# Two attention layers and an MLP on one core: pinning VectorE's waits, setting a PSUM tile aside earlier, and cutting filler work finer

## The chip, the cores and the metric

The kernel runs on one core of a Trainium2 chip. The metric is the time of one execution on the device, in microseconds. Before the change it is 3975.42 us, the median of three runs (3967.12, 3975.87 and 3975.42).

## What is computed

Sixteen images of 256 channels by 32x32 positions, all in fp32. Each goes through two blocks in turn; S = 1024 positions are the tokens.

```
layer 0:  qkv = xs @ w_proj + b_proj                 # 4 heads of 64
          attn = softmax(q k^T * 64**-0.5)
          x = (attn v) @ w_out + b_out + xs
layer 1:  h = group_norm(x)                          # 32 groups of 8 channels
          q, k, v = h @ qkv_w^T                      # 8 heads of 32
          attn = softmax(q k^T * 32**-0.5 + phys_bias)
          x = x + (attn v) @ proj_w^T + proj_b
          h = group_norm(x)
          x = x + mlp_w2 @ gelu(mlp_w1 @ h + mlp_b1) + mlp_b2     # 256 -> 1024 -> 256
```

The softmax is computed without subtracting a maximum: the kernel sums the exponentials, checks at the end that no denominator left a safe range, and would run a slower general pass if one had (it does not with these inputs). A weighted sum of v is scaled by the reciprocal of the denominator afterwards.

## The kernel before

An image lives in SBUF as two chunks of 128 channels by 1024 positions. Positions are taken in two halves of 512 (`TB`, index `t`), keys in eight blocks of 128 (`kb`).

**The first attention** (`attention_a`) has four items: two halves `t` by two pairs of heads `c`. Each item has eight units, one for each key block. A unit computes scores (`s_a`, line 296, four matmuls of 64x64 side by side), the exponential on ScalarE (`e_a`, line 304), and two units later the weighted sum (`acc_a`, line 318, four matmuls). VectorE adds up the exponentials (`es_a`, line 330) for the denominators. **The second attention** (`attention_b`) also has four items of eight units: scores of four heads (`s_b`, line 401, eight matmuls of 32x64), two exponentials (`e_b`, line 413), the weighted sum one unit later (`acc_b`, line 422, four matmuls of 128x32) and two additions on VectorE (`es_b`, line 439).

**PSUM.** Accumulators of even items, of the second attention, and its denominators come from a pool of two single banks (`bank`). Everything else comes from three tiles of two banks each, s0 to s2, handed out in turn by `wide`: scores, projections, pieces of qkv and MLP, group norm averages, denominators of the first attention. A new tile waits until all readers of the old one in the same place are done. The sums of the odd items of the first attention (`acc_a_1`, `acc_a_3`) take tile 2 as a whole: from their first `weigh` until their last, `kept` holds the number 2 and `wide` passes over it. By then the scores of the item's first three units have been handed out from all three tiles.

**Denominators.** `normalise` forms column sums with matmuls (`den_a`, line 348; `den_b`, line 454). `denominators` then copies them to SBUF on ScalarE (`d`), spreads them over partitions with a DMA (`sp`), takes reciprocals on VectorE (line 262), writes them to DRAM (`row`) and reads them back broadcast over partitions (`rd`). VectorE multiplies the weighted sums by what came back (lines 367 and 469), after which the output projection `o` or `j` can run.

**Order of work.** The program is written as one stream. A small planner, `Later`, holds functions that fall due after a number of steps; it ticks once for each unit or piece. `run` steps through an attention and may run one filler piece after a unit, from the dictionary `fill`. In an image the order is: first attention; first MLP product (`hidden`, m<-gn_h, line 676) of the image before; the first half of q and k and all of v of the second attention; second attention, with filler pieces between its units: the rest of q and k (4 pieces at units 0, 1, 2, 4), the second MLP product of the image before (`reduce`, m<-g; 8 pieces, each 8 products over 256 positions), and q, k, v of the next image's first attention (12 pieces). During attentions `product` cuts a 128-column matmul into four of 32 columns (`cols`), which run side by side. The group norm before the MLP (`gm_h`, `gv_h`, lines 533 to 565) of an image falls into the next image's first attention, with the second output projection `j_1` ahead of it.

A scheduler under the kernel then fixes the order of instructions in each engine's queue. It keeps the dependencies, but may put an instruction ahead of others on its engine when it takes its input to be ready sooner, DMA transfers included. Waits are semaphores set by the producing engine.

Names used below: `x` the image (updated in place), `res_a`, `res_b` the weighted sums, `rd_a`, `rd_b` the transferred reciprocals, `sp_a`, `sp_b` the spread denominators, `inv` their reciprocals, `mean_c`, `dv`, `tv`, `rstd` steps of the group norm, `gn_g`, `gn_h` its two results.

Of the kernel before, what the change touches and what calls it, by code (L numbers as in the profile page):

```python
# [188 lines left out]
def first_pass(ctx, tc, x, out, k):  # L189
    nc = tc.nc  # L190
    B, C, S = x.shape
    CC, SB, NT = C // P, S // P, S // TB
    HC = k["w1"].shape[2] // P
    later = Later()
# [8 lines left out]
        tc.tile_pool(name="ps_a", bufs=2, space=bass.MemoryType.PSUM)  # L203
    )


    turn, kept = [0], set()

    dram = ctx.enter_context(
        tc.tile_pool(name="dram", bufs=4, space=bass.MemoryType.DRAM)  # L210
    )

    def wide(name, n=None):
        while n is None:
            if turn[0] not in kept:
                n = turn[0]
            turn[0] = (turn[0] + 1) % 3
        return ps_s.tile([P, 2, TB], F32, tag=f"s{n}", name=name)

    def bank(name):  # L220
# [29 lines left out]

    def denominators(key, d, n, waits, then):
        w = 4 * TB // P
        spread = work.tile([P, w], F32, tag="spread", name=f"sp_{key}", bufs=2)
        row = dram.tile([4 * TB // n, n], F32, tag="row", name=f"row_{key}", bufs=4)
        full = work.tile([P, CC * TB], F32, tag="full", name=f"rd_{key}", bufs=1)[:, :n]
        nc.sync.dma_start(spread, d[::32].rearrange("p (a b) -> p a b", b=w))

        def invert():  # L260
            inverse = work.tile([P, w], F32, tag="inverse", name=f"inv_{key}", bufs=2)
            nc.vector.reciprocal(inverse, spread)
            nc.sync.dma_start(row.rearrange("r (a b) -> (r a) b", b=w), inverse)
            nc.gpsimd.tensor_add(dsum, dsum, spread)
            nc.gpsimd.tensor_add(isum, isum, inverse)
            num = P * n // (4 * TB)
            for r in range(P // num):
                nc.sync.dma_start(
                    full[r * num : (r + 1) * num], row[r].partition_broadcast(num)
                )  # L270
            later.after(waits[1], lambda: then(full))

        later.after(waits[0], invert)
# [10 lines left out]
    def attention_a(b, qT, kT, v, project):  # L284
        key, D, lag = f"a_{b}", D0, 2
        items = [(t, c) for t in range(NT) for c in range(CC)]
        units = [(i, kb) for i in range(len(items)) for kb in range(SB)]
        res = act.tile([P, CC, S], F32, tag="res", name=f"res_{key}")
        accs, held, sums = {}, {}, {}

        def scores(i, kb):
            t, c = items[i]
            s = wide(f"s_{key}_{i}_{kb}")
            for g in range(2):
                for h in range(0, P, HALF):
                    nc.tensor.matmul(  # L296
                        s[h : h + HALF, g, :],
                        kT[g * D : (g + 1) * D, c, kb * P + h : kb * P + h + HALF],
                        qT[g * D : (g + 1) * D, c, t * TB : (t + 1) * TB],
                        start=True,  # L300
                        stop=True,
                    )
            e = work.tile([P, 2, TB], F32, tag="e", name=f"e_{key}_{i}_{kb}", bufs=8)
            nc.scalar.activation(e, s, AF.Exp, scale=float(D) ** -0.5)  # L304
            return i, kb, e

        def weigh(i, kb, e):
            t, c = items[i]
            if kb == 0:
                if i % 2:  # L310
                    kept.add(2)
                    acc = wide(f"acc_{key}_{i}", 2)
                    accs[i] = [acc[:, h, :] for h in range(2)]
                else:
                    accs[i] = [bank(f"acc_{key}_{i}_{h}") for h in range(2)]
            for h in range(2):
                for g in range(2):
                    nc.tensor.matmul(  # L318
                        accs[i][h][g * D : (g + 1) * D, :],
                        v[h * HALF : (h + 1) * HALF, kb, c * 2 + g],  # L320
                        e[h * HALF : (h + 1) * HALF, g, :],
                        start=(kb == 0),
                        stop=(kb == SB - 1),
                    )
            if kb == 0:
                held[i] = e
                return
            if kb == 1:
                sums[i] = work.tile([P, 2, TB], F32, tag="es", name=f"es_{key}_{i}", bufs=4)
            nc.vector.tensor_add(sums[i], held[i] if kb == 1 else sums[i], e)  # L330
            if kb == SB - 1:
                r = res[:, c, t * TB : (t + 1) * TB]
                one, two = accs.pop(i)
                nc.scalar.copy(r, one)
                nc.vector.tensor_add(r, r, two)  # L335
                kept.discard(2)
                if c == CC - 1:
                    later.after(1, lambda: normalise(t))


        def normalise(t):
            half = TB // 2
            den = wide(f"den_{key}_{t}")[:, 0, :]
            for c in range(CC):
                for g in range(2):
                    for h in range(2):
                        j = (2 * g + h) * 32
                        nc.tensor.matmul(
                            den[j : j + 32, c * half : (c + 1) * half],
                            k["ones"][:, :32],  # L350
                            sums[t * CC + c][:, g, h * half : (h + 1) * half],
                            start=True,
                            stop=True,
                        )
            denominators(
                f"{key}_{t}", den_copy(f"{key}_{t}", den), CC * TB,
                (2, 5) if t < NT - 1 else (1, 1),
                lambda full: scale(t, full),
            )

        def scale(t, full):
            r = res[:, :, t * TB : (t + 1) * TB]
            halves = [
                y.rearrange(form, c=CC, h=2)
                for y, form in ((r, "p c (h q) -> p c h q"), (full, "p (h c q) -> p c h q"))
            ]
            nc.vector.tensor_mul(halves[0], *halves)
            later.after(1 if t < NT - 1 else 4, lambda: project(t, res))

        cols[0] = 32  # L370
        pending = []
        for n, u in enumerate(units):
            pending.append(scores(*u))
            if n >= lag:
                weigh(*pending.pop(0))
            yield
        for p in pending:
            weigh(*p)
            if p is pending[-1]:
                cols[0] = P  # L380
            yield

# [5 lines left out]
    def attention_b(b, qT, kT, v, project):  # L388
# [5 lines left out]
        accs, held, sums = {}, {}, {}  # L394
# [55 lines left out]
        def normalise(i, r, last):  # L450
            t, c = items[i]
            den = bank(f"den_{key}_{i}")
            for g in range(G):
# [6 lines left out]
                )  # L460
            denominators(
                f"{key}_{i}", den_copy(f"{key}_{i}", den), TB,
                ((3, 5) if b + 1 < B else (1, 1)) if last else (2, 2),
                lambda full: scale(i, r, last, full),
            )

        def scale(i, r, last, full):
            t, c = items[i]
            nc.vector.tensor_mul(r, r, full)
            if c == CC - 1:  # L470
                wait = (10 if b + 1 < B else 1) if last else 1
                later.after(wait, lambda: project(t, res[t]))
# [195 lines left out]


    def mlp(b, xb, hn):  # L670
        gs = {}

        def hidden(t, hc):
            ps = wide(f"m1_{b}_{t}_{hc}")[:, 0, :]
# [9 lines left out]
            nc.scalar.activation(g, ps, AF.Gelu, bias=k["m1b"][:, hc : hc + 1])  # L684
            gs[t, hc] = g

        def reduce(t, co, half):
            n = TB // 2
            ps = wide(f"m2_{b}_{t}_{co}_{half}")[:, 0, :n]
            for hc in range(HC):  # L690
                product(
                    ps,
                    k["w2"][:, hc, co * P : (co + 1) * P],
# [1 line left out]
                    start=(hc == 0),  # L695
                    stop=(hc == HC - 1),
                )
            y = xb[:, co, t * TB + half * n : t * TB + (half + 1) * n]
            nc.vector.scalar_tensor_tensor(  # L699
                y, ps, k["m2b"][:, co : co + 1], y, ALU.add, ALU.add  # L700
            )
            if half:
# [5 lines left out]
        return (  # L708
            [lambda t=t, hc=hc: hidden(t, hc) for t in range(NT) for hc in range(HC)],
            [  # L710
                lambda t=t, co=co, half=half: reduce(t, co, half)
                for t in range(NT) for co in range(CC) for half in range(2)
            ],
        )


    def run(stage, fill=None):
        for n, _ in enumerate(stage):
            later.tick()
            if fill and n in fill:  # L720
                fill[n]()

    def run_pieces(pieces):
        for piece in pieces:
            piece()
            later.tick()

# [24 lines left out]
    for b in range(B):  # L754
# [16 lines left out]
        later.flush()  # L771
        tiles1, (qk, v) = qkv_1(b, xn[0])
        n = len(qk) // CC
        run_pieces(qk[:n] + v)
        fill = dict(zip((0, 1, 2, 4), qk[n:]))
        rest = outputs + (first if b > 0 else [])
        end = []
        if b == B - 1:

            rest, end = rest[:4], rest[4:]  # L780
        for m, piece in enumerate(rest):
            fill[5 + m * (last - 5) // (len(rest) - 1)] = piece
        hn = []
        run(
            attention_1(
# [312 lines left out]
```

## Time and profile before

| | |
|---|---|
| span of the profiled execution | 3973.2 us |
| TensorE (PE) busy | 3894.5 us, 98% |
| VectorE (DVE) busy | 2121.3 us, 53% |
| ScalarE (ACT) busy | 2044.0 us, 51% |
| mean granted TensorE clock | 0.995 |
| one image in the middle (476.53 to 722.89) | 246.36 us |
| of it: first attention, MLP's first product, front of qkv, second attention | 71.79, 31.51, 13.86, 129.20 us |

How to read it: the busy time of TensorE is the union of its matmuls' durations, and a matmul of which the end is modelled may seem to last until the next starts. The starts are exact, so a stage is best read by the distance of the starts of its groups. In a timeline, a row has start, duration, engine, line, operation, output<-inputs, tile of the array (rows*columns), shape and the number of records merged; in brackets stands the idle time before it and what ended it. One fp32 matmul appears as two records. Groups that run on different parts of the array overlap, so the durations of records add up to more than the time. "PEld" rows are weight loads, which run beside matmuls. In the list of waits a row has the engine, the waiting instruction, what it waited for, the total, the count and the longest.

### The profile page before, as it was taken

The numbers are of one execution on the slowest core, as the hardware profiler recorded it, in microseconds if no ns is written. First come the engines' busy times: TensorE is split into PE (matmuls) and PEld (weight loads), VectorE is DVE, ScalarE is ACT, GpSimd is POOL, SyncE is SP. The second block draws the span as 40 slices with busy tenths as digits, with TensorE's granted clock in tenths as the row PEclk, the third lists the DMA queues.
The fourth block names the chain that finished last, engine by engine and source line by source line (L and its number), as shares of the span: only waits on it lengthen the run. The fifth ranks groups of instructions, "written<-read, shape, count | busy, mean of one in ns | idle before, by whom it ended". The sixth has DMA issues, their size and how long they took to land.

```text
span 3973.2 us, 84589 instructions
## 1 busy us (share of the span) xinstructions
PE 3894.5 (98%) x37485; PEld 1461.6 (37%) x37485; DVE 2121.3 (53%) x2569; ACT 2044.0 (51%) x2369; POOL 93.9 (2%) x252
## 2 busy tenths in 40 slices
PE   8999999999999999999999999999999999999998
PEld 3324343343433434334333343433434334343335
DVE  4573645636456464564645546455464554645562
ACT  4654645546455464554645446454464544646461
POOL 1000000000000000000000000000000000000000
PEclk9999999999999999999999999999999999999999
DMA  2000000000000000100000000000000100000000
GB/s 81 12 12 15 26 12 28 12 17 23 12 29 15 15 23 12 31 15 12 23 12 31 15 16 20 12 32 15 25 15 7 31 15 26 15 9 18 15 12 23
DMA packets 62436, 78.39 MB, mean 20 GB/s; under 512 B 35344, under 2 KB 36880, under 8 KB 62064
## 3 DMA queue, kind: packets, MB, share of 16 engines
q1 hardware_dynamic: 57728, 68.72, 5.9%
q8 instruction: 295, 4.83, 0.5%
q10 hardware_dynamic: 3712, 3.80, 0.3%
q14 instruction: 77, 0.63, 0.1%
q0 software_dynamic: 624, 0.41, 0.0%
HBM read 54.54 MB, written 17.56 MB: 18 GB/s over the span
## 4 chain that ended last, share of the span: by engine, by line
PE 92%; DMA 3%; DVE 3%; issue 1%; ACT 1%; SPq 0%; POOL 0%; DVEq 0%; POOLq 0%; ACTq 0%
PE s_b L401 14%; PE acc_b L422 12%; PE m L676 11%; PE m L242 11%; PE acc_a L318 10%; PE s_a L296 9%; PE qk_b L242 6%; PE qk_a L242 5%; PE o L242 3%; PE v_a L242 3%; PE v_b L242 3%; PE j L242 3%; PE den_b L454 2%; DMA rd_a<-row_a 1%; ACT e_a L304 1%
## 5 line engine op out<-in xcount | busy, mean ns | idle before, releaser
L413 ACT ACTIVATE e_b<-s_b 128x1024 f32<-128x1024 f32 x1024 | 994.7, 1024 | 673.4 <-PE s_b L401 666.5
L439 DVE TENSOR_TENSOR es_b<-es_b,e_b 128x1024 f32<-128x1024 f32 x768 | 897.6, 1219 | 309.9 <-ACT e_b L413 309.8
L304 ACT ACTIVATE e_a<-s_a 128x1024 f32<-128x1024 f32 x512 | 520.9, 1024 | 475.8 <-PE s_a L296 474.3
L318 PE MATMUL acc_a<-e_a,v 64*64 64x512 f32 x4096 | 674.2, 597 | 9.4 <-ACT e_a L304 9.4
L296 PE MATMUL s_a<-q,k 64*64 64x512 f32 x4096 | 683.2, 601 | 0.2 <-DVE res_a L335 0.2
L401 PE MATMUL s_b<-q,k 32*64 32x512 f32 x8192 | 594.1, 613 | 3.4 <-DVE x L699 3.4
L422 PE MATMUL acc_b<-e_b,v 128*32 128x512 f32 x4096 | 546.1, 604 | 0.1
L330 DVE TENSOR_TENSOR es_a<-es_a,e_a 128x1024 f32<-128x1024 f32 x384 | 469.7, 1223 | 138.5 <-ACT e_a L304 129.8
L242 PE MATMUL m<-g,w 128*32 128x256 f32 (+1 forms) x7616 | 463.9, 379 | 2.7 <-DVE x L500 2.7
L676 PE MATMUL m<-gn_h,w 128*128 128x512 f32 x1024 | 455.2, 599 | 2.2 <-DVE gn_h L562 2.2
L242 PEld LDWEIGHTS m<-g,w 128*32 128x32 f32 (+1 forms) x7616 | 277.9, 112 | 218.1 <-issue 66.7
L684 ACT ACTIVATE g<-m,m1b 128x512 f32<-128x512 f32 x256 | 175.9, 687 | 329.1 <-PE m L676 329.1
L318 PEld LDWEIGHTS acc_a<-e_a,v 64*64 64x64 f32 x4096 | 215.8, 134 | 317.0 <-issue 231.1
L296 PEld LDWEIGHTS s_a<-q,k 64*64 64x64 f32 x4096 | 208.6, 135 | 273.5 <-issue 192.8
L676 PEld LDWEIGHTS m<-gn_h,w 128*128 128x128 f32 x1024 | 190.4, 191 | 234.3 <-issue 218.7
L439 DVE TENSOR_TENSOR es_b<-e_b,e_b 128x1024 f32<-128x1024 f32 x128 | 151.1, 1221 | 234.1 <-ACT e_b L413 234.1
L401 PEld LDWEIGHTS s_b<-q,k 32*64 32x64 f32 x8192 | 142.2, 129 | 358.4 <-issue 197.4
L242 PE MATMUL qk_a<-x,wp 128*32 128x512 f32 (+1 forms) x1856 | 244.5, 594 | 9.2 <-DMA wp<-in_L_conv_w_proj_dram 6.9
L242 PE MATMUL qk_b<-gn_g,wq 128*32 128x512 f32 (+1 forms) x1280 | 234.4, 593 | 0.0
L422 PEld LDWEIGHTS acc_b<-e_b,v 128*32 128x32 f32 x4096 | 82.3, 108 | 406.8 <-issue 402.5
L606 DVE TENSOR_TENSOR v<-v_b,eones 128x512 f32<-128x512 f32 x64 | 44.2, 691 | 291.3 <-PE v_b L242 291.3
L699 DVE SCALAR_TENSOR_TENSOR x<-m,m2b,x 128x256 f32<-128x256 f32 x128 | 61.8, 483 | 155.6 <-PE m L242 155.5
(111 smaller groups left out, 2038.3 us busy)
## 6 DMA issues: line engine op xcount, KB each, us to landing
x<-in_x_dram SPq DMA_DIRECT2D x32, 512.0 KB
rd_a<-row_a SPq DMA_DIRECT2D x64, 256.0 KB
rd_b<-row_b SPq DMA_DIRECT2D x256, 64.0 KB
out_dram<-x SPq DMA_DIRECT2D x64, 256.0 KB
w<-in_L_conv_mlp_w_dram ACTq DMA_DIRECT2D x2, 1024.0 KB
sp_b<-d_b SPq DMA_DIRECT2D x64, 8.0 KB
row_b<-inv_b SPq DMA_DIRECT2D x64, 8.0 KB
wq<-in_L_conv_qkv_w_dram ACTq DMA_DIRECT2D x1, 768.0 KB
```

The costliest lines, as they stand in the source:

```text
L242: nc.tensor.matmul(o[sl], w[:, sl], r, **flags)
L296: nc.tensor.matmul(s[h : h + HALF, g, :], kT[g * D : (g + 1) * D, c, kb * P + h : kb * P + h + HALF], qT[g * D : (g + 1) * D, c, t * TB : ...
L304: nc.scalar.activation(e, s, AF.Exp, scale=float(D) ** -0.5)
L318: nc.tensor.matmul(accs[i][h][g * D : (g + 1) * D, :], v[h * HALF : (h + 1) * HALF, kb, c * 2 + g], e[h * HALF : (h + 1) * HALF, g, :], st ...
L330: nc.vector.tensor_add(sums[i], held[i] if kb == 1 else sums[i], e)
L401: nc.tensor.matmul(tiles[g // 2][h : h + HALF, g % 2, :], kT[g * D : (g + 1) * D, c, kb * P + h : kb * P + h + HALF], qT[g * D : (g + 1) * ...
L413: nc.scalar.activation(e, s, AF.Exp, scale=float(D) ** -0.5)
L422: nc.tensor.matmul(accs[i][g * D : (g + 1) * D, :], v[:, kb, c * G + g], es[g // 2][:, g % 2, :], start=(kb == 0), stop=(kb == SB - 1),)
L439: nc.vector.tensor_add(d, held[i][n] if kb == 1 else d, e)
L454: nc.tensor.matmul(den[g * D : (g + 1) * D, :], k["eones"][:, c * G + g], sums[i][g // 2][:, g % 2, :], start=True, stop=True,)
L676: nc.tensor.matmul(ps, k["w1"][:, cc, hc * P : (hc + 1) * P], hn[0][:, cc, t * TB : (t + 1) * TB], start=(cc == 0), stop=(cc == CC - 1),)
L684: nc.scalar.activation(g, ps, AF.Gelu, bias=k["m1b"][:, hc : hc + 1])
```

## The change

It has three parts.

- Three VectorE operations that read what a DMA brought, the reciprocal and the two multiplies, are pinned in VectorE's queue behind everything that the program issued to VectorE before them (`keep_in_program_order`). This adds no wait; it keeps the scheduler from placing them earlier. Later instructions may still move ahead of them.
- Tile 2 is set aside for the sums of an odd item from the item's first scores, not from its first weighing. `wide` hands out the tile used longest ago among those not set aside, in place of strict turns.
- The filler of the second attention is spread more evenly. A piece of the second MLP product is cut in two halves over the inner dimension, which fall on different units; the first half leaves its PSUM tile set aside until the second is done. Three of the four pieces of v move from ahead of the second attention into it. Several pieces may share a unit, and one more place, after the last scores, takes pieces. In the second attention, reciprocals of all items but the last are due one step earlier and the multiply one step later (waits (2, 2) become (1, 3)).

```diff
-    turn, kept = [0], set()
+    order, kept = [0, 1, 2], set()
+
+    def use(n):
+        order.remove(n)
+        order.append(n)
 
     def wide(name, n=None):
-        while n is None:
-            if turn[0] not in kept:
-                n = turn[0]
-            turn[0] = (turn[0] + 1) % 3
+        if n is None:
+            n = next(m for m in order if m not in kept)
+        use(n)
         return ps_s.tile([P, 2, TB], F32, tag=f"s{n}", name=name)
...
-            nc.vector.reciprocal(inverse, spread)
+            tc.keep_in_program_order(nc.vector.reciprocal(inverse, spread))
...
         def scores(i, kb):
             t, c = items[i]
+            if kb == 0 and i % 2:
+                kept.add(2)
             s = wide(f"s_{key}_{i}_{kb}")
...
             if kb == 0:
                 if i % 2:
-                    kept.add(2)
                     acc = wide(f"acc_{key}_{i}", 2)
...
-                kept.discard(2)
+                if i % 2:
+                    kept.discard(2)
...
-            nc.vector.tensor_mul(halves[0], *halves)
+            tc.keep_in_program_order(nc.vector.tensor_mul(halves[0], *halves))
...
-                ((3, 5) if b + 1 < B else (1, 1)) if last else (2, 2),
+                ((3, 5) if b + 1 < B else (1, 1)) if last else (1, 3),
...
-            nc.vector.tensor_mul(r, r, full)
+            tc.keep_in_program_order(nc.vector.tensor_mul(r, r, full))
...
-        def reduce(t, co, half):
+        def reduce(t, co, half, part):
             n = TB // 2
-            ps = wide(f"m2_{b}_{t}_{co}_{half}")[:, 0, :n]
-            for hc in range(HC):
+            if part == 0:
+                held.append(wide(f"m2_{b}_{t}_{co}_{half}")[:, 0, :n])
+                kept.add(order[-1])
+                slot.append(order[-1])
+            else:
+                use(slot[-1])
+                kept.discard(slot.pop())
+            ps = held[-1]
+            for hc in range(part * HC // 2, (part + 1) * HC // 2):
...
     def run(stage, fill=None):
         for n, _ in enumerate(stage):
+            pieces = fill.get(n, ()) if fill else ()
+            if n > last:
+                run_pieces(pieces, False)
             later.tick()
-            if fill and n in fill:
-                fill[n]()
...
-        run_pieces(qk[:n] + v)
-        fill = dict(zip((0, 1, 2, 4), qk[n:]))
+        run_pieces(qk[:n] + v[:1])
+        own = [v[1], qk[n], v[2], qk[n + 1], v[3], *qk[n + 2 :]]
+        fill = {m: [piece] for m, piece in enumerate(own)}
         rest = outputs + (first if b > 0 else [])
         end = []
         if b == B - 1:
 
-            rest, end = rest[:4], rest[4:]
+            rest, end = rest[:8], rest[8:]
         for m, piece in enumerate(rest):
-            fill[5 + m * (last - 5) // (len(rest) - 1)] = piece
+            at = len(own) + m * (last + 1 - len(own)) // max(1, len(rest) - 1)
+            fill.setdefault(at, []).append(piece)
```

More of the change, by code (lines that the diff above doesn't have):

```diff
@@ L373, in attention_a @@
             pending.append(scores(*u))
+            if n == len(units) - 1:
+                break
             if n >= lag:
@@ L376, in attention_a @@
             yield
-        for p in pending:
-            weigh(*p)
-            if p is pending[-1]:
+        while pending:
+            weigh(*pending.pop(0))
+            if not pending:
                 cols[0] = P
@@ L670, in mlp @@
     def mlp(b, xb, hn):
-        gs = {}
+        gs, held, slot = {}, [], []
         def hidden(t, hc):
@@ L697, in reduce @@
                 )
+            if part == 0:
+                return
             y = xb[:, co, t * TB + half * n : t * TB + (half + 1) * n]
@@ L710, in mlp @@
             [
-                lambda t=t, co=co, half=half: reduce(t, co, half)
+                lambda t=t, co=co, half=half, part=part: reduce(t, co, half, part)
                 for t in range(NT) for co in range(CC) for half in range(2)
+                for part in range(2)
             ],
@@ L718, in run, with run_pieces @@
         for n, _ in enumerate(stage):
+            pieces = fill.get(n, ()) if fill else ()
+            if n > last:
+                run_pieces(pieces, False)
             later.tick()
-            if fill and n in fill:
-                fill[n]()
-    def run_pieces(pieces):
+            if n <= last:
+                run_pieces(pieces, False)
+    def run_pieces(pieces, tick=True):
         for piece in pieces:
             piece()
-            later.tick()
+            if tick:
+                later.tick()
     xs = {0: load_x(0)}
```

## The prediction

> **What bounds the kernel now.** I read the page first, then the list of waits, then the timelines of TensorE (PE) and VectorE (DVE) in one image in the middle, 967 to 1214 us.
>
> ```profile
> PE 3894.5 (98%) x37485; PEld 1461.6 (37%) x37485; DVE 2121.3 (53%) x2569; ACT 2044.0 (51%) x2369; POOL 93.9 (2%) x252
> PE 92%; DMA 3%; DVE 3%; issue 1%; ACT 1%; SPq 0%; POOL 0%; DVEq 0%; POOLq 0%; ACTq 0%
> ```
>
> TensorE sets the end: 98% busy, 92% of the chain. So only what TensorE loses can be won. But "busy" hides losses, because ends of matmuls are modelled; I therefore go by starts. A clean group of the first attention (8 records of 64x64 tiles, four side by side) starts every 0.858 us (1005.51, 1006.37, 1007.23 in the timeline). At that rate, 0.427 us for 512 columns of the whole array, all matmul records add up to 3578 us (each record's share of rows, columns and length, summed). Some 395 us of 3973 are thus lost, and they repeat from image to image. Where, by starts: first attention 8.2 us an image over images 1 to 15 (6.9 to 10.0), MLP's first product 0.8, the qkv front 0.2, second attention 13.1 us in each of images 1 to 14.
>
> The list of waits names two of the causes (engine, line, waited for, total us, times, longest):
>
> ```profile
> PE gv_h L519 <- DVE tv_h L542: 41.6, 15, 3.8
> PE acc_a L318 <- ACT e_a L304: 9.4, 32, 0.3
> PEld s_b L401 <- ACT e_b L413: 112.3, 134, 0.8
> ```
>
> 15 times is once an image, 32 twice, 134 some eight times an image plus image 0 and 15. The timeline of PE and DVE at the first:
>
> ```profile
> 1012.43 1.10 PE L318 MATMUL acc_a<-e_a,v 64*64 64x512 f32 x8
> 1016.64 0.27 PE L519 MATMUL gv_h<-tv_h,gavg 64*64 64x2 f32 x2 [3.11 <-DVE tv_h L542]
> ...
> 1016.88 1.95 PE L296 MATMUL s_a<-q,k 64*64 64x512 f32 x6
> 1018.42 1.74 PE L318 MATMUL acc_a<-e_a,v 64*64 64x512 f32 x8
> ```
> ```profile
> 1008.53 1.23 DVE L330 TENSOR_TENSOR es_a<-es_a,e_a 128x1024 f32<-128x1024 f32 x1 [0.49 <-ACT e_a L304]
> 1013.40 1.22 DVE L367 TENSOR_TENSOR res_a<-res_a,rd_a 128x1024 f32<-128x1024 f32 x1 [3.65 <-DMA rd_a<-row_a]
> 1014.54 1.22 DVE L330 TENSOR_TENSOR es_a<-es_a,e_a 128x1024 f32<-128x1024 f32 x1
> 1015.68 0.32 DVE L536 COPY mean_h<-gm_h 64x2 f32<-64x2 f32 x2
> ```
>
> VectorE stands 3.65 us at the multiply by transferred reciprocals; the group norm's small steps queue behind it, and TensorE waits for the last of them, tv_h. Then eight records take 1.5 us instead of 0.86: the granted clock was halved for 3.4 us. By the trace's clock record such a dip follows nine of the fifteen gaps.
>
> **What the Trainium skill says.** "PSUM — Partial Sum Buffer", section "Engine vs sequencer instructions": VectorE's and ScalarE's queues are strict first in, first out, and matmuls keep their order. The gap above agrees: copies whose input was ready since 1010 started at 1015.68. "TensorE: Matmul & The Clock Gate", Part 1: the clock falls to half when the array is idle and recovers after about 3.4 us of activity; the dips after the gaps agree (3.4 us at 0.5). "TensorEngine Tiling (Array Packing)", "Key Properties": a change of tiling mode drains TensorE. Agrees: entering other tile shapes costs 0.12 to 0.19 us below. "DMA: Bandwidth & Descriptors", the anatomy section, puts about 2 us fixed on a DMA (for another issuing path); here sp_a's lands 1.9 us after issue (1003.68 to the first reader at 1005.62).
>
> **Part 1, the pins (L262, L367, L469).** Durations don't change (1.22, 0.69 and 0.25 us); only places in the queue. In the built programs' order, before has es_a(2,4), multiply, es_a(2,5), mean_h, dv, dv, tv; the changed one es_a(2,5), mean_h, dv, dv, tv, es_a(2,6), multiply. What now stands ahead of what TensorE needs is the reciprocal, ahead of "x += j". I count from the end of acc_a(1,7), T: den_a copied by T+1.8, its DMA 1.9 us, so the reciprocal ends near T+4.0; j starts at T+2.2 (part 2) and takes 3.5, so nothing waits for the reciprocal. Then x+=j, statistics and mean_c take 3.0 us (1002.16 to 1005.12) with es_a(2,2) among them: T+10.2. Three more es_a at 1.22 us, the last held by its exponential to T+12.8; then 0.9 us of small steps: tv_h ends near T+15.0, and gv_h comes up on TensorE near T+15.8. Slack 0.8 us: the gap closes. The multiply comes up near T+16 with its data there since about T+11 (6.9 us from reciprocal to landing before); o_0 needs it at T+19. **Gain**: 15 gaps of 3.0 us (starts, 45.3 in all) and 9 dips of 1.7 us: 60 us.
>
> **Part 2, tile 2 set aside at the item's scores, least recently used first.** The 32 waits of 0.3 us look small, but starts show more: 14 s_a records from 983.23 with acc_a not before 985.41, and from there groups run broken (x1, x3, x4) to the item's end. The first odd item's 16 groups take 983.23 to 998.45, 15.22 us against 13.73 (16 x 0.858); the second's 14 take 13.56 against 12.01. The cause is that scores(1,0) to (1,2) may still hold tile 2 when the sums want it, so the scheduler put s_a(i,3) half ahead. In the changed program s_a and acc_a alternate in fours there. **Gain**: 3.0 us an image, 16 images: 49 us. Two tiles suffice for scores: a tile is wanted again 2.6 us after its last matmul, an exponential takes 1.02 after 0.2. **Cost**: j_1 now gets the least recently used tile, which is the sums' own, and must wait for ScalarE's copy and VectorE's add (2.2 us after acc_a ends: 998.45 to 1000.64 before). den_a, moved ahead of j_1, fills 1.0 us of it and the first quarter of s_a(2,2) a little more, so 0.9 us an image stays. Bounds 0 and 2.2; I take 0.9, 15 times: 14 us lost.
>
> **Part 3, fill of the second attention.** Timeline, a unit being s_b, acc_b, fill:
>
> ```profile
> 1094.11 1.90 PE L242 MATMUL qk_b<-gn_g,wq 128*32 128x512 f32 x16
> 1095.94 1.11 PE L401 MATMUL s_b<-q,k 32*64 32x512 f32 x16
> 1096.98 1.06 PE L422 MATMUL acc_b<-e_b,v 128*32 128x512 f32 x8
> 1097.98 1.28 PE L401 MATMUL s_b<-q,k 32*64 32x512 f32 x16
> 1099.19 1.06 PE L422 MATMUL acc_b<-e_b,v 128*32 128x512 f32 x8
> 1100.07 1.90 PE L242 MATMUL qk_b<-gn_g,wq 128*32 128x512 f32 x16
> 1101.90 1.11 PE L401 MATMUL s_b<-q,k 32*64 32x512 f32 x16
> 1102.94 1.07 PE L422 MATMUL acc_b<-e_b,v 128*32 128x512 f32 x8
> 1103.83 3.64 PE L242 MATMUL m<-g,w 128*32 128x256 f32 x64
> 1107.39 1.11 PE L401 MATMUL s_b<-q,k 32*64 32x512 f32 x16
> ```
>
> With fill, acc_b and s_b take 0.89 + 1.04; without, 1.00 + 1.21: TensorE waits for ScalarE's two exponentials (2.05 us a unit). An empty unit costs 0.29 us. Before, 24 fills lie on 32 units, eight are empty; after, 35 pieces (3 v, 4 qk, 16 halves, 12 of the next image) leave none. Eight x 0.29 = 2.3 us. Against it: a whole piece takes 3.56, two halves 2 x 1.83, 0.1 each, seven pairs apart: 0.7; three v pieces in tiles of 32 columns 0.09 dearer each: 0.3. The last v piece now stands ahead of den_b_3, which before took 1.53 instead of 0.86 us: 0.67 won. Net 2.0 us, images 1 to 14: **28 us**. Image 0 (4 fills before, 7 after) gives some 1 us. Image 15 (8 before, 15 after) I put at nothing: seven fewer empty units give 2 us, but a half piece's tile is then held over three units, leaving scores two tiles, which takes as much.
>
> The held tile costs nothing elsewhere: with a fill in every unit, scores used the same two tiles already, wanted 2.6 us after s_b ends, exponentials done at 2.3. The reciprocal one unit sooner (waits 1,3) may stop VectorE for some 1.5 us four times an image; VectorE has 75.4 busy us of 129.2 there, and the MLP tile behind it is wanted again over 4 us later. Nothing taken.
>
> **Sum.** 60 + 49 - 14 + 28 + 1 = 124: 3975 - 124 = 3851 us.
>
> **Rivals.** (a) A new wait replaces the gap: the transfer sp_a lands late (VectorE waited up to 2.3 us for it), x+=j slips, gv_h still waits about 2 us. Then 30 us of gaps, the 15 us of dips, and some 5 us more at j_1: 3900. For it: slack is only 0.8 us. Against: landing 1.9 us in both windows read. Chance 0.12. (b) Nothing waits at j_1 and the remaining changes of tile order help too: 3851 - 14 - 10 = 3827. Chance 0.10. (c) Slower: the pinned reciprocals hold VectorE for the longest wait seen (4.2 us), four times an image, and the MLP's eviction behind passes over half to TensorE: 0.55 x 4.2 x 4 x 15 = 140 us, 3990. Against: VectorE's slack, and the reciprocal waited 1.7 us on average already (101.0 over 58). Chance 0.05. Fills cancelled by drains and only the gaps won, 3975 - 60 = 3915: 0.04. All cancelled, 3975: 0.02. The forecast's own case: 0.67.
>
> Range 3825 to 3900: from (b) to (a). Faster by over 0.3%: 0.93; within: 0.02; slower: 0.05.
>
> **What would show it.** The waits list without PE gv_h, without PE acc_a on e_a at 32, and with PEld s_b on e_b far below 134; granted clock above 0.997; VectorE's multiply behind tv_h; a new PE wait of j for DVE res_a, about 15 times; second attention near 132 us an image with three v pieces inside, first attention near 65. It would be wrong if gv_h still waited, or if s_b or the MLP pieces began to wait for VectorE's x.

## The result, and the profile after

The changed kernel takes **3877.6 us** (median of four runs, 3877.4 to 3879.3) against 3975.0 us for the kernel before on the same chip: ratio 0.976, 95% interval 0.9743 to 0.9777. That is 97 us less. The forecast was 124 us less, 3851, in a range from 3825 to 3900.

The changed kernel's page, first the busy times, then the chain by engine:

```profile
PE 3846.9 (99%) x38637; PEld 1435.3 (37%) x38637; DVE 2116.0 (55%) x2569; ACT 2048.2 (53%) x2369; POOL 84.8 (2%) x252
```
```profile
PE 92%; DVE 5%; ACT 1%; issue 1%; DMA 0%; POOL 0%; ACTq 0%; SPq 0%; DVEq 0%
```

TensorE (PE) still sets the end, with 1152 matmuls more (halved pieces don't add any; three v pieces an image in tiles of 32 columns do). Its granted clock is 1.000 (0.995 before). The list of waits, engine, line, waited for, total us, times, longest:

```profile
PE m L685 <- DVE mean_g L545: 3.8, 15, 0.3
PE j L246 <- DVE res_a L341: 3.0, 15, 0.2
```
```profile
PEld s_b L410 <- ACT e_b L422: 133.6, 159, 1.1
```

gv_h's 41.6 us and the 32 waits of acc_a for e_a are gone. The waits that have come instead look tiny; the starts below show that they are not. The timeline of VectorE (DVE) where it stood for 3.65 us before:

```profile
984.12 0.16 DVE L551 TENSOR_TENSOR tv_h<-dv_h,mv_h 128x2 f32<-128x2 f32 x1
984.20 1.22 DVE L336 TENSOR_TENSOR es_a<-es_a,e_a 128x1024 f32<-128x1024 f32 x1
985.34 1.22 DVE L374 TENSOR_TENSOR res_a<-res_a,rd_a 128x1024 f32<-128x1024 f32 x1
```

The multiply now stands behind tv_h and finds its data there: no idle time before it. tv_h ends at 984.28, and TensorE comes to gv_h only at 985.31:

```profile
985.31 0.16 PE L528 MATMUL gv_h<-tv_h,gavg 64*64 64x2 f32 x1
```

TensorE around the end of the first odd item:

```profile
968.08 1.04 PE L324 MATMUL acc_a<-e_a,v 64*64 64x512 f32 x8
969.04 1.07 PE L355 MATMUL den_a<-es_a,ones 128*32 128x256 f32 x16
970.04 1.07 PE L303 MATMUL s_a<-q,k 64*64 64x512 f32 x2
971.32 3.64 PE L246 MATMUL j<-res_b,wpj 128*32 128x512 f32 x32 [0.21 <-DVE res_a L341]
974.89 0.65 PE L303 MATMUL s_a<-q,k 64*64 64x512 f32 x3
974.91 0.64 PE L324 MATMUL acc_a<-e_a,v 64*64 64x512 f32 x1
```

Eights of s_a and acc_a alternate every 0.86 us to the item's end. But two records of s_a, worth 0.21 us, take the 1.28 us from 970.04 to 971.32: j waits there for the sums' tile, and most of the wait hides in the modelled end of s_a. After j the groups are out of step again.

"Lost" below is the time by starts beyond 0.427 us for 512 columns of the whole array, as in the prediction, in all 16 images:

| stage | before | after | saved |
|---|---|---|---|
| first attention | 129.0 | 51.7 | 77.3 |
| MLP's first product | 12.4 | 24.4 | -12.0 |
| qkv front and second attention | 229.2 | 198.6 | 30.6 |

The sum is 95.9 us. The rest is the kernel's start: the first score comes at 33.6 us before and at 31.8 after, and over the traces of all runs it comes between 31.3 and 33.8, whatever was changed.

### The profile page after: what moved, and what is told of

Same layout as the page of the kernel before. It is cut to its first block, busy times and chain, and to the rows that moved or that the text cites. A ratio compares the mean times of both kernels' runs of the same rounds, so it can differ in the third digit from the quotient of the medians.

```text
span 3875.7 us, 86863 instructions
## 1 busy us (share of the span) xinstructions
PE 3846.9 (99%) x38637; PEld 1435.3 (37%) x38637; DVE 2116.0 (55%) x2569; ACT 2048.2 (53%) x2369; POOL 84.8 (2%) x252
## 4 chain that ended last, share of the span: by engine, by line
PE 92%; DVE 5%; ACT 1%; issue 1%; DMA 0%; POOL 0%; ACTq 0%; SPq 0%; DVEq 0%
PE s_b L410 14%; PE acc_b L431 13%; PE m L685 12%; PE m L246 11%; PE s_a L303 10%; PE acc_a L324 9%; PE qk_b L246 6%; PE qk_a L246 6%; PE v_b L246 3%; PE v_a L246 3%; PE j L246 3%; DVE es_a L336 2%; PE o L246 2%; PE den_b L463 1%; ACT e_a L311 1%
## 5 line engine op out<-in xcount | busy, mean ns | idle before, releaser
L410 PE MATMUL s_b<-q,k 32*64 32x512 f32 x8192 | 581.4, 613 | 1.2 <-DVE x L509 0.6
L303 PE MATMUL s_a<-q,k 64*64 64x512 f32 x4096 | 562.1, 593 | 2.4 <-DVE x L509 2.4
L324 PE MATMUL acc_a<-e_a,v 64*64 64x512 f32 x4096 | 555.1, 589 | 0.0
L246 PE MATMUL m<-g,w 128*32 128x256 f32 (+1 forms) x7616 | 482.7, 379 | 0.3 <-DVE mean_h L545 0.3
L324 PEld LDWEIGHTS acc_a<-e_a,v 64*64 64x64 f32 x4096 | 183.2, 133 | 260.9 <-issue 233.0
L303 PEld LDWEIGHTS s_a<-q,k 64*64 64x64 f32 x4096 | 167.3, 133 | 280.6 <-issue 207.2
L410 PEld LDWEIGHTS s_b<-q,k 32*64 32x64 f32 x8192 | 126.0, 129 | 307.8 <-ACT e_b L422 133.6
L246 PEld LDWEIGHTS qk_b<-gn_g,wq 128*32 128x32 f32 (+1 forms) x1280 | 81.9, 126 | 137.4 <-issue 127.8
```

Source lines behind the costliest of these rows:

```text
L246: nc.tensor.matmul(o[sl], w[:, sl], r, **flags)
L303: nc.tensor.matmul(s[h : h + HALF, g, :], kT[g * D : (g + 1) * D, c, kb * P + h : kb * P + h + HALF], qT[g * D : (g + 1) * D, c, t * TB : ...
L324: nc.tensor.matmul(accs[i][h][g * D : (g + 1) * D, :], v[h * HALF : (h + 1) * HALF, kb, c * 2 + g], e[h * HALF : (h + 1) * HALF, g, :], st ...
L410: nc.tensor.matmul(tiles[g // 2][h : h + HALF, g % 2, :], kT[g * D : (g + 1) * D, c, kb * P + h : kb * P + h + HALF], qT[g * D : (g + 1) * ...
```

## The experiments

P stands for the three pins, T for the order of tiles (set aside early, least recently used first), F for the finer fill. Ratios are to the kernel before.

| run | P | T | F | us | ratio (95%) |
|---|---|---|---|---|---|
| e10_onepin | first attention's multiply | | | 3915.3 | 0.985 (0.983 to 0.9863) |
| e1_pins | yes | | | 3907.2 | 0.983 (0.981 to 0.9847) |
| e2_tile | | yes | | 3902.5 | 0.982 (0.9799 to 0.9837) |
| e3_fill | | | yes | 4107.3 | 1.034 (1.0314 to 1.0357) |
| e9_nofill | yes | yes | | 3899.3 | 0.981 (0.9791 to 0.9824) |
| e6_nopins | | yes | yes | 3911.6 | 0.984 (0.9825 to 0.9857) |
| e5_turns | yes | set aside early, but in turns | yes | 3988.7 | 1.003 (1.002 to 1.0045) |
| e7_late | yes | least recently used, but set aside late | yes | 3895.4 | 0.979 (0.9778 to 0.981) |
| the change | yes | yes | yes | 3877.6 | 0.976 (0.9743 to 0.9777) |
| e4_release | yes | and counted as used when freed | yes | 3855.3 | 0.970 (0.9677 to 0.9714) |
| e8_recent | yes | and the tile used last set aside | yes | 3847.0 | 0.968 (0.9661 to 0.9694) |
| e11_last | yes | as e8 | whole pieces in image 15 | 3842.7 | 0.966 (0.9646 to 0.9678) |

**The pins alone** (e1), put into the kernel before:

```diff
-            nc.vector.reciprocal(inverse, spread)
+            tc.keep_in_program_order(nc.vector.reciprocal(inverse, spread))
...
-            nc.vector.tensor_mul(halves[0], *halves)
+            tc.keep_in_program_order(nc.vector.tensor_mul(halves[0], *halves))
...
-            nc.vector.tensor_mul(r, r, full)
+            tc.keep_in_program_order(nc.vector.tensor_mul(r, r, full))
```

> The kernel before with the three pins alone. Forecast's part 1: the wait of gv_h for tv_h goes, with the half-clock dips behind it: 60 us (15 x 3.0 + 9 x 1.7), so 3915 us, and the granted clock goes to 0.999 or more. Rival: the 27 us that the whole change fell short of the forecast are missing here, because the pinned reciprocal ahead of x += j makes a new wait: then some 3940 us, and gv_h or gm_h still waits for VectorE.

3907.2 us. The first attention lost 70.1 us instead of 129.0, so the gap and its clock dips were worth 58.9 us. A further 10 us came from the second attention of image 0 (22.3 to 17.9) and of image 15 (19.5 to 13.8); the fourteen between stayed at 13.1 each.

**The first attention's multiply alone pinned** (e10), the middle pair of lines of that diff, in the kernel before:

> The kernel before with one pin of the three, the first attention's multiply by transferred reciprocals. Theory 'the gap before gv_h is this multiply's alone, and the other two pins gave their 10 us in the second attention of images 0 and 15': first attention as with all three pins (70 us lost in 16 images), time 3915 us. Rival 'the unpinned reciprocal takes its place at the head of VectorE's queue': 3930 us or more.

3915.3 us, as the first theory said: the first attention lost 70.2, the second attention 226.8 (225.8 before). So this multiply is the whole gap, and the other two pins gave the 10 us in images 0 and 15.

**The order of tiles alone** (e2):

```diff
-        while n is None:
-            if turn[0] not in kept:
-                n = turn[0]
-            turn[0] = (turn[0] + 1) % 3
+        if n is None:
+            n = next(m for m in order if m not in kept)
+        use(n)
...
             t, c = items[i]
+            if kb == 0 and i % 2:
+                kept.add(2)
             s = wide(f"s_{key}_{i}_{kb}")
```

> The kernel before with tile 2 set aside at the scores and the tile used longest ago handed out, nothing else. Forecast's part 2: 49 us won in the odd items, 14 us lost at j: 3940 us. Theory from the trace after: handing out the tile used longest ago gives j the sums' own tile and moves den_a behind a piece of the MLP, which costs j's wait (1.06 us), groups out of step behind j (0.5 us) and waits in the MLP's first product (0.75 us) an image, and the odd items win only 2.4 us: some 4 us in all, so 3965 to 3975 us, with the gap at gv_h still there.

3902.5 us: both missed, on the same side. The gap at gv_h is gone without a pin, and the first attention loses 45.9 us instead of 129.0. VectorE's timeline in this run:

```profile
988.86 1.22 DVE L372 TENSOR_TENSOR res_a<-res_a,rd_a 128x1024 f32<-128x1024 f32 x1
990.00 2.55 DVE L334 TENSOR_TENSOR es_a<-es_a,e_a 128x1024 f32<-128x1024 f32 x2
992.46 0.32 DVE L541 COPY mean_h<-gm_h 64x2 f32<-64x2 f32 x2
```

The multiply still stands ahead of mean_h, but it doesn't wait. With j held back by the sums' tile, den_a stands ahead of j on TensorE, a whole j (3.6 us) sooner. Counted from the end of the first odd item's acc_a, the transfer `rd_a` is issued after 5.4 us here (983.12) and after 9.5 before (1007.95), while VectorE comes to the multiply at nearly the same time, after 11.1 and 11.3 us. The data has landed by then. Parts 1 and 2 therefore close the same gap, each by itself.

**The finer fill alone** (e3), with turns and without pins:

```diff
-            for hc in range(HC):
+            for hc in range(part * HC // 2, (part + 1) * HC // 2):
...
-        run_pieces(qk[:n] + v)
-        fill = dict(zip((0, 1, 2, 4), qk[n:]))
+        run_pieces(qk[:n] + v[:1])
+        own = [v[1], qk[n], v[2], qk[n + 1], v[3], *qk[n + 2 :]]
+        fill = {m: [piece] for m, piece in enumerate(own)}
```

> The kernel before with the filler work alone (halved MLP pieces with their tile kept, three pieces of v inside, several pieces to a unit, waits 1 and 3); tiles still in turns, tile 2 set aside at the first weighing, no pins. Forecast's part 3: 29 us, so 3946 us. By the stages of the trace after (30.6 us): 3944 us. Rival: half pieces need the other parts of the change, since without pins the multiplies block VectorE where the MLP tiles' evictions are queued: 3960 us or more.

4107.3 us, 130 us slower than the kernel before on the same chip: on the rival's side, and far above its 3960. The second attention lost 358 us instead of 226. Its waits of TensorE:

```profile
PE s_b L406 <- DVE x L713: 27.8, 57, 2.5
PE m L244 <- DVE x L713: 20.5, 15, 2.9
```

x at line 713 is VectorE's eviction of an MLP piece. Two things could delay TensorE there: s_b getting the tile of the half just finished, or VectorE held by an unpinned multiply ahead of the eviction. The next two runs take one each.

**The change with tiles in turns** (e5), pins and early set-aside kept:

```diff
-        if n is None:
-            n = next(m for m in order if m not in kept)
-        use(n)
+        while n is None:
+            if turn[0] not in kept:
+                n = turn[0]
+            turn[0] = (turn[0] + 1) % 3
+        given[0] = n
```

> The changed kernel with the three tiles handed out strictly in turns, as before, instead of least recently used first; the early set-aside, the pins and the finer fill stay. Theory 'the fill needs the new order' (with turns the next scores or the next MLP piece get the tile that was used last, because the held tile is passed over, so TensorE waits for VectorE's x or ScalarE's e_b): second attention some 8 to 13 us an image longer than in the changed kernel, as in the run with the fill alone: 3990 to 4080 us. Rival 'the fill alone was slow because VectorE's queue was held by unpinned multiplies': near 3880 us, with the second attention near 132.7 us an image.

3988.7 us: the first theory, just below its lower end. The second attention lost 19.9 us an image instead of 11.5. The wait of s_b is there as often as in e3, with pinned multiplies:

```profile
PE s_b L408 <- DVE x L715: 20.0, 57, 0.8
```

TensorE around one second half, in this run:

```profile
1108.50 1.91 PE L244 MATMUL m<-g,w 128*32 128x256 f32 x32
1110.34 1.79 PE L408 MATMUL s_b<-q,k 32*64 32x512 f32 x16
```

s_b starts 1.72 us apart from what follows (1110.34 to 1112.06 for acc_b), elsewhere 1.04. In one image seven of its s_b groups lose 0.9 to 2.0 us, while in the changed kernel 31 of 32 lose 0.2. So of the 358 us that e3 lost in the second attention, the pins and the early set-aside take off 42 (316 here), and the order of tiles the next 120 (196 in the changed kernel).

**The change without its pins** (e6):

> The changed kernel without its three pins. Theory 'the order of tiles already closes the gap, since den_a stands ahead of j': near 3878 us, within 10 us of the changed kernel, with no wait of gv_h for tv_h. Rival 'the pins carry the gap and the fill': 3940 to 3990 us, with gv_h waiting again or VectorE held at the second attention's multiply by rd_b.

3911.6 us, 34 us above the changed kernel: between the two. The first theory is right for the first attention, which has no gap and loses 45.9 us, less than with the pins (51.7). Most of that difference is one score an image: in the changed kernel it waits 0.34 us for o's eviction, because the pinned multiply runs behind tv_h and VectorE comes to that eviction 4.1 us after o begins (989.01 to 993.13); here it is 3.7 us (999.94 to 1003.65), and the score doesn't wait. The first theory is wrong for the second, which loses 235.0 instead of 196.2. The waits of VectorE and of TensorE that appear there (TensorE's s_b waits for x 7 times as well, 6.5 us), and VectorE's timeline:

```profile
DVE res_b L478 <- DMA rd_b<-row_b: 130.6, 64, 3.8
```
```profile
PE m L246 <- DVE x L718: 12.7, 12, 1.9
```
```profile
1104.56 0.69 DVE L478 TENSOR_TENSOR res_b<-res_b,rd_b 128x512 f32<-128x512 f32 x1 [2.94 <-DMA rd_b<-row_b]
1105.17 2.35 DVE L448 TENSOR_TENSOR es_b<-es_b,e_b 128x1024 f32<-128x1024 f32 x2
1107.44 0.48 DVE L718 SCALAR_TENSOR_TENSOR x<-m,m2b,x 128x256 f32<-128x256 f32 x1
```

The unpinned multiply waits for its transfer 64 times, 2 us on average (3 times, 2.1 us in all, in the changed kernel). The eviction behind it runs late: the MLP piece that TensorE left at 1104.58 is taken out at 1107.44, and the next piece stands 1.28 us for its tile, until 1107.97. The queue is first in, first out, as the Trainium skill says in "PSUM — Partial Sum Buffer", section "Engine vs sequencer instructions", and this trace agrees: the eviction starts only behind the multiply and the two additions. The kernel before, whose multiplies are unpinned too, has nearly the same waits (58 times, 105.9 us), but there the pins changed nothing in images 1 to 14 (e1). So in those images the waits cost only together with the finer fill. Images 1 to 14 take 134.2 to 135.9 us each here; with the pins all fourteen take 132.67.

**The change without the finer fill** (e9):

> The kernel before with the pins, the early set-aside and the least-recently-used order, but with whole MLP pieces and all v pieces ahead of the second attention, as before. Forecast's part 3 (2.0 us an image and 1 us in image 0, 29 us in all): 3906 us. Rival 'the finer fill gives nothing of its own': 3878 us. The runs of pins alone (3907) and tile order alone (3903) are near it if both close the same gap: then pins and tile order together give hardly more than either.

3899.3 us, so the fill is worth 21.7 us given the rest. It lies below e1 and e2 by only 8 and 3 us, as the overlap of pins and tile order demands.

**Set aside late again** (e7): `kept.add(2)` back at the item's first weigh, the rest as in the change.

> The changed kernel with tile 2 set aside only at the first weigh of an odd item, as before; least recently used order, pins and fill stay. Theory 'the least-recently-used order alone makes the odd items alternate, since tile 2 is then handed out early enough before the sums begin': within 5 us of the changed kernel, 3873 to 3883 us. Rival 'the early set-aside does it': the 32 waits of acc_a for e_a return and the time is 3910 us or more.

3895.4 us, between the two, and for a reason that neither had:

```profile
PE acc_a L323 <- DVE x L507: 15.8, 16, 1.0
```

The 32 waits for e_a don't come back, so the new order alone lets the odd items alternate. The early set-aside alone does it too: e5, with tiles in turns, has none of these waits either. But once an image the projection o lands in tile 2 before the item's sums claim it, and the sums wait 1.0 us for o's eviction. With the early set-aside a score of the item gets that tile, later. The first attention lost 68.4 us, 16.7 more than in the change.

**The sums' tile counted as used when it is freed** (e4), so that j_1 no longer gets it:

```diff
                 if i % 2:
                     kept.discard(2)
+                    use(2)
```

> The changed kernel with one line more: when the sums of an odd item are finished, tile 2 is noted as the one used last, so that j and den_a get tiles of scores instead. Theory (the order of tiles is where the 27 us went): j no longer waits for VectorE's res_a, j stands ahead of den_a again, den_a(1) ahead of the MLP's pieces, and about 2.2 us an image come back: 3843 to 3850 us. Rival (two tiles for the scores of odd items cost it): the wait of s_a for x stays and little changes, 3868 us or more.

3855.3 us, between the two. The wait of j is gone, den_a stands behind j again and the MLP's first product loses 12.8 us instead of 24.4. A new wait comes:

```profile
PE s_a L303 <- DVE rstd_h L559: 13.2, 15, 1.4
```

Item 3's second score block takes the tile of gv_h, which VectorE has not read yet.

**The tile used last set aside** (e8), which for item 3 is gv_h's own:

```diff
             if kb == 0 and i % 2:
-                kept.add(2)
+                aside.append(order[-1])
+                kept.add(aside[-1])
...
                 if i % 2:
-                    kept.discard(2)
+                    use(aside[-1])
+                    kept.discard(aside.pop())
```

> The changed kernel, with the tile for an odd item's sums chosen as the one used last when that item's scores begin (instead of always tile 2), and counted as used when the sums are done. Theory 'the changed kernel still pays for j's wait at the sums' tile, and the run that freed it late paid instead 0.9 us an image where s_a takes gv_h's tile and waits for VectorE's rstd_h': both waits vanish from the list, and the time is 13 us below that run: 3840 to 3846 us. Rival 'something else holds s_a there': 3855 us or more.

3847.0 us, 1 us above the expected stretch. Both waits are gone, and TensorE's timeline at the end of the odd item is whole:

```profile
959.73 1.04 PE L325 MATMUL acc_a<-e_a,v 64*64 64x512 f32 x8
960.70 3.64 PE L246 MATMUL j<-res_b,wpj 128*32 128x512 f32 x32
964.16 1.04 PE L357 MATMUL den_a<-es_a,ones 128*32 128x256 f32 x16
965.13 1.09 PE L304 MATMUL s_a<-q,k 64*64 64x512 f32 x8
```

First attention and MLP's first product together lose 44.7 us (76.1 in the change).

**Whole pieces in image 15** (e11), on top of e8: both halves of an MLP piece in one unit of that image's second attention.

```diff
         for m, piece in enumerate(rest):
+            if b == B - 1:
+                m -= m % 2
             at = len(own) + m * (last + 1 - len(own)) // max(1, len(rest) - 1)
```

> The run with the most recently used tile set aside, and in image 15 alone both halves of an MLP piece in one unit of the second attention, so that no tile is held across units there. Theory 'image 15 loses 5 us to the held half, which leaves scores two tiles for three units (s_b starts 2.00 us apart instead of 1.28)': 5 us less, 3842 us, and the second attention of image 15 loses 14 us instead of 19. Rival 'empty units cost the same there': 3847 us.

3842.7 us, 4.3 less, and image 15 loses 15.2 us in its second attention instead of 18.8 (14 expected). What it removes is seen in the changed kernel, where a half's tile is held and a unit has no fill:

```profile
3737.86 2.00 PE L410 MATMUL s_b<-q,k 32*64 32x512 f32 x16
3739.80 1.06 PE L431 MATMUL acc_b<-e_b,v 128*32 128x512 f32 x8
...
3747.65 1.28 PE L410 MATMUL s_b<-q,k 32*64 32x512 f32 x16
```

The first half of a piece ran at 3733.79 and the second follows at 3743.77. Between them scores have two tiles, and the second s_b of that stretch takes 1.94 us (3737.86 to 3739.80). Behind the second half they have three again, and the second s_b takes 1.21 (3747.65 to 3748.86). This is the fastest of all versions run.

## Why the prediction was right, and where a term was off

The direction and the range held, and the waits that the prediction named are gone. The sum was 27 us too large. Part 2 brought 29 us less than forecast, and part 3 brought 9 us less; that the latter hardly shows in the sum is luck, since the pins gave 10 us at a place where none were forecast.

**Part 1: forecast 60, measured 58.9** (first attention, e1). The working held: tv_h 1.0 us ahead of gv_h on TensorE where 0.8 was forecast, and no dips left. One reading was off: by the clock record eight of the fifteen gaps are followed by a dip, not nine; the ninth dip (227.8 us) stands at the end of image 0's second attention. With eight the sum is 45.3 + 13.6 = 59. Two things were missed. The pins also gave 10 us in the second attention of images 0 and 15. And e2 shows that the gap isn't the pins' own: part 2 closes it too, since its den_a stands ahead of j. Part 2's step put den_a ahead of j_1 only to fill j's wait; that it also sends the transfer off 4 us earlier wasn't followed to the multiply. Given part 2, the pins win nothing in the first attention (45.9 us lost without them, 51.7 with them); what they are worth in the changed kernel lies in the second, with its finer fill (235.0 without, 196.2 with).

**Part 2: forecast 49 - 14 = 35, measured 6.4** (first attention and MLP's first product, 82.5 lost in e1, 76.1 in e9). Two terms of the sum were mis-sized.
- The odd items: 49 forecast, 37.8 measured, which is what e8 wins over e1 (82.5 to 44.7) where j pays nothing. I took both odd items down to the clean rate. In the changed kernel they still take 13.84 us (955.20 to 969.04) and 12.56 us (992.58 to 1005.14), against 13.73 and 12.01 at that rate: 2.4 us saved an image, not 3.0. Part of the rest is the score that waits for o's eviction, 0.33 us by starts (993.49 to 994.68 for a group worth 0.86); it waits in e8 too.
- The cost of j: 14 forecast, 31.4 measured (76.1 against 44.7 in e8). The 0.9 us an image at j itself was about right: 1.06 by starts. Left out was what follows from the new order: 12.0 of the 31.4 us are lost in the MLP's first product (24.4 against 12.4), and 0.2 us an image where s_a and acc_a are out of step behind j (974.89 to 976.59, 1.70 us for 14 records worth 1.50). I had bounded the wait and not the order behind it. The sum lands almost at my upper bound of 2.2 us an image (33 us). By starts the 12.0 us, 0.75 an image, have two places. At gm_g the next MLP piece comes after 0.53 us instead of 0.14: this is the wait of m for mean_g in the list above, which shows 0.25 of it. And den_a_1 now stands behind the first MLP piece, which costs 0.36 us; 0.15 of that was lost in the first attention before. In e5, with tiles in turns, j waits as it does in the change, but the MLP's first product loses only 12.4. So it is the order by last use that costs here, not j's wait.

**Part 3: forecast 29, measured 20.2** given pins and tile order (218.8 lost in e9, 198.6 in the change), and 21.7 by time. Images 1 to 14 gave 1.7 us each against 2.0 forecast, 24 us in all. Image 0 gave the 1 us. Image 15, put at nothing, lost 5 us: the held halves cost more there than seven empty units, and e11, without them, wins 3.6 us of it back. Against the kernel before the stages show 30.6, close to the 29, but only because 10 us of the pins lie in the same stages. "Nothing taken" for the held tile and for the earlier reciprocal was right only for the change as a whole: with tiles in turns the fill costs 8.4 us more an image (e5), and without the pins 39 us in all (e6). No run takes the earlier reciprocal by itself; by the code the multiply falls due at the same step as before (1 + 3 against 2 + 2), later only as counted from its reciprocal.

Together: 58.9 + 6.4 + 20.2 + 10 = 95.5 us of the 97.

**The rivals.** (a) A new wait at gv_h did not come. (c) had its mechanism the wrong way round: it is the unpinned multiplies that hold VectorE and delay the MLP's eviction (e6), not the pinned reciprocals, which wait as much with pins as without (58 times, 104 us in both). (b), that nothing waits at j_1, is what e8 brings about, and its gain of 24 was sized too low: e8 lies 31 us below the change.

**The signs.** Right: gv_h and the 32 waits gone, clock 1.000, the multiply behind tv_h, j's 15 waits for res_a, first attention 65.4 us and second 132.7. Wrong: PEld s_b on e_b rose from 134 to 159 times although the stage lost less. Weight loads run beside matmuls, and these waits did not show in the time of the stage.

## What to carry to other kernels

Size a wait by the starts of the groups around it, not by the list: 15 waits of 0.2 us at j and 15 of 0.3 at an MLP piece, with the loss around them, cost 31 us. When a buffer wait moves an instruction, follow everything that is now ahead of it and behind it, transfers included; here that closed one gap for free and opened another loss. Parts of one change are not a sum: the finer fill costs 130 us by itself and brings 22 us with the pins and the tile order, and before setting a buffer aside ask who gets each of the others next.

## What was not expected

A half piece's held tile is free where every unit has a fill, and in image 15, where units between the halves have none, it costs some 0.9 us a piece (e11 wins 3.6 us with four pieces); 0.7 of that is one s_b (1.94 us against 1.21). In the changed kernel the second attention repeats to 0.01 us (132.67 us in fourteen images running); without the pins (e6) it varies by 1.7 us from image to image. It did not vary like that in the kernel before, where the same multiplies are unpinned (13.1 to 13.2 us lost in each of those images).
